# Sums of the density with one factor taken out, and x added on GpSimd, in an attention-then-density kernel

## The chip, the cores and the metric

The kernel runs on one core of a Trainium2 chip. A core has five engines that work side by side, each through its own instructions in order: TensorE (PE; its weight loads are shown as PEld), VectorE (DVE), ScalarE (ACT), GpSimd (POOL) and SyncE (SP), which here issues the DMAs. They wait for each other through semaphores. The metric is the device time of one execution in microseconds; less is better.

## The reference

x has 8 images of 192 channels and 64 x 64 points. Two layers follow each other, each added to x after a group norm (32 groups). The first is attention over the 4096 points of an image, the second a density per channel: a small network of four layers, applied to the normed value less 0.5 and plus 0.5, whose two results give a likelihood.

```python
def _L0_conv_ref(x, w1, b1, a1, w2, b2, a2, wa, ba, aa):
    q, k, v = prelu(conv1x1(x, w1, b1), a1), prelu(conv1x1(x, w2, b2), a2), prelu(conv1x1(x, wa, ba), aa)
    score = softmax(einsum("bnc,bcm->bnm", q, k), axis=2)      # 4096 x 4096 for each image
    return einsum("bnm,bmc->bnc", score, v)

def _logits_cumulative(logits, ms, bs, fs):                    # filters 1, 3, 3, 3, 1 per channel
    for i in range(4):
        logits = einsum("cij,cjn->cin", softplus(ms[i]), logits) + bs[i]
        if i < 3:
            logits = logits + tanh(fs[i]) * tanh(logits)
    return logits

def _L1_conv_ref(x, ...):
    lower, upper = _logits_cumulative(xr - 0.5, ...), _logits_cumulative(xr + 0.5, ...)
    sign = -sign(lower + upper)
    return maximum(abs(sigmoid(sign * upper) - sigmoid(sign * lower)), 1e-6)

x = x + _L0_conv_ref(_gn(x), ...)
x = x + _L1_conv_ref(_gn(x), ...)
```

## The kernel before

**Attention.** An image is cut into 8 blocks of 512 queries, and each block into 16 steps of 256 keys, so an image has 128 steps and the main loop 1024 (`for t in range(last)`). A step issues, in this order: the products and the max-reduce of a step 21 ahead (`max_step`: two matmuls of L753 into the one PSUM tile `mx`, and the reduce L761 on VectorE), the exponential on ScalarE of the next step's scores (L824, L829), and the eight products with the values (`attend`, L840). The next image's norm, keys and values are made in the same steps (`prepare`), and the density of the image before runs beside them. Keys pass through ScalarE and VectorE, then their difference is taken on GpSimd (L613, half as wide as a density piece) and SP stores both to HBM.

**Density.** A tile has 128 partitions and 1024 points. An image makes 12 units (`Unit`): two column blocks c, three channel groups g, two signs s (lower and upper). A unit of images 0 to 6 runs, with tiles from 17 shared buffers:
- `tanh0` (three tanhs of x, L1097) and `linear` (the three linear sums of x of layer 1, L1106) on ScalarE;
- `mix` (9 multiply-adds on VectorE), `tanh` (L1112) and `gate` (3);
- for each of three sums of layer 2: `scaled` on ScalarE (L1122, factor times the first input, plus bias) and `more` twice on VectorE, then tanh, and later the gate;
- for layer 3 `scaled`, one `more`, and `plain` (L1154) on ScalarE, whose result GpSimd adds in two half tiles (L1160).

All multiply-adds but one kind go through the helper `stt`, so they share the line L1129. When both units of a tile are through, `ending` takes the sum, the tanhs (L1354), a sign (L1356), the difference and the product with the sign on GpSimd (L1350, L1362, L1370, in half tiles), the magnitude on ScalarE (L1404), and adds to x on VectorE (L1409).

**Order.** No scheduler of the compiler is used; the program writes the order itself. `density_step` hands out density instructions in each step by planned costs: a rate for VectorE, worked out from the multiply-adds that are left and the steps that are left, and limits by step. It gives an instruction out only when what it needs was given out in an earlier step. GpSimd's half-tile operations wait in the list `pieces`; `pool_step` takes one out in each step and puts a tiny memset (`pause`, L1315) in front, which waits for the last helper multiply-add but one (`recent`), so that the piece runs beside the reduce.

**Tail.** The density of the last image (`on_pe`) runs after the loop, ordered by `tail_step` with planned clocks. The sums of layer 1 are matmuls with diagonal matrices (L1068: three tanhs and x with diagonals of `diagonals` and `linear_diagonals`; `fill` puts x into a bank by ScalarE instead, L1052), then `tanh1` and `gate1` (L1087); layers 2 and 3 are as above. An ending there is all on VectorE and ScalarE (`alone`).

`parameters` works out the constants of the network, one small VectorE operation a step during image 0, and `norm_end` scales them by an image's norm.

Of the kernel before, what the change touches and what calls it, by code (L numbers as in the profile page):

```python
# [18 lines left out]
def kernel(  # L19
# [213 lines left out]
    wx = const.tile([128, 3, 2, 3], F32, name="wx")  # L233
    bx = const.tile([128, 2, 3, 2, 3], F32, name="bx")

    def parameters():
# [30 lines left out]
        yield  # L267
        nc.scalar.activation(tf, ff, AF.Tanh)
# [25 lines left out]
        nc.vector.tensor_copy(wx[:, :, 0, :], wsp[:, :, 0:3])  # L294
        yield
        nc.vector.tensor_copy(wx[:, :, 1, :], la)
        yield
        for i, k in enumerate((-0.5, 0.5)):
            nc.vector.scalar_tensor_tensor(
                bx[:, i, :, 0, :], wsp[:, :, 0:3], k, cb[:, :, 0:3], ALU.mult, ALU.add  # L300
            )
            yield
            nc.vector.scalar_tensor_tensor(bx[:, i, :, 1, :], la, k, lb, ALU.mult, ALU.add)
            yield
# [133 lines left out]
    def norm_end(key, n, t, then=None):  # L438
# [41 lines left out]
        def fourth():  # L480

            res, ve, sq = cell["res"], cell["ve"], cell["sq"]
            rq = small.tile([128, 1], F32, tag="rq", name=f"rq_{nm}")
            nc.vector.reciprocal(rq, sq)
            nc.vector.tensor_tensor(rq, rq, ve, ALU.mult)
            nc.vector.tensor_tensor(rq, rq, sq, ALU.add)
            nc.vector.tensor_scalar(rq, rq, 0.5, None, ALU.mult)
            nc.vector.reciprocal(res[:, 1:2], rq)
            norms[key] = res
            if key[1] == 1:  # L490

                nmr = small.tile([128, 1], F32, tag="nmr", name=f"nmr_{nm}")
                nc.vector.scalar_tensor_tensor(
                    nmr, res[:, 0:1], -1.0, res[:, 1:2], ALU.mult, ALU.mult
                )
                wn = small.tile([128, 3, 2, 3], F32, tag="wn", name=f"wn_{nm}")
                nc.vector.tensor_scalar(wn, wx, res[:, 1:2], None, ALU.mult)
                bn = small.tile([128, 2, 3, 2, 3], F32, tag="bn", name=f"bn_{nm}")
                for i in range(2):
                    nc.vector.scalar_tensor_tensor(  # L500
                        bn[:, i].rearrange("p a b c -> p (a b c)"),
                        wx.rearrange("p a b c -> p (a b c)"), nmr,
                        bx[:, i].rearrange("p a b c -> p (a b c)"), ALU.mult, ALU.add,
                    )
                norms[key] = wn, bn
            if then:
                then()
# [407 lines left out]
    COST = {"DVE": 1.22, "ACT": 1.23, "TANH": 1.05}  # L915
# [6 lines left out]
    lower2 = mm.rearrange("p g n -> p (g n)")[:, 0:36].rearrange("p (s g i) -> p s g i", s=4, g=3)  # L922

    def diagonals(g, t):

        def one(k):
            if k == 0:
                d = vtiles.pop(0).rearrange("p a b c -> p (a b c)")[:, 0 : 12 * 128]
                diag.append(d.rearrange("p (k n) -> p k n", k=12))
            nc.scalar.activation(diag[g][:, k, :], ident, AF.Copy, scale=lc[:, g, k : k + 1])  # L930
# [4 lines left out]
    def linear_diagonals(b, g):  # L935
        wn, bn = norms[b, 1]
        for i in range(3):
            nc.scalar.activation(
                diag[g][:, 9 + i, :], ident, AF.Copy, scale=wn[:, g, 1, i : i + 1]
            )  # L940

    def tail(b):
        wn, bn = norms[b, 1]

        for s in range(2):
            d, q = lower2[:, s], lower2[:, 2 + s]
            nc.vector.tensor_copy(d, cb[:, :, 6:9])
            for j in range(3):
                nc.vector.tensor_tensor(
                    q, wsp[:, :, 12 + j : 21 : 3],  # L950
                    bn[:, s, :, 1, j : j + 1].to_broadcast([128, 3, 3]), ALU.mult,
                )
                nc.vector.tensor_tensor(d, d, q, ALU.add)
# [7 lines left out]
    class Unit:  # L961
# [3 lines left out]
        def __init__(self, b, c, g, s):  # L965
# [29 lines left out]
            else:  # L995
                for i in range(3):
                    add("ACT", ("t", 0, i), [], self.tanh0, makes="t")
                    add("ACT", ("l", 1, i), [], self.linear, makes="l")
                for i in range(3):
                    for j in range(3):  # L1000
                        add(
                            "DVE", ("mix", i, j), [("t", 0, j), ("l", 1, i)], self.mix,
# [5 lines left out]
            for i in range(3):  # L1008
                add("ACT", ("l", 2, i), [("gate", 1, 0)], self.scaled, makes="l")
                for j in (1, 2):  # L1010
                    add("DVE", ("add", 2, i, j), [("gate", 1, j), ("l", 2, i)], self.more)
                add("ACT", ("t", 2, i), [("add", 2, i, 2)], self.tanh, makes="t")
            for i in range(3):
                add("DVE", ("gate", 2, i), [("t", 2, i)], self.gate, frees=[("t", 2, i)])
            add("ACT", ("l", 3, 0), [("gate", 2, 0)], self.scaled, makes="z")
            add("DVE", ("add", 3, 0, 1), [("gate", 2, 1), ("l", 3, 0)], self.more)
            if self.on_pe:
                add("DVE", ("add", 3, 0, 2), [("gate", 2, 2), ("l", 3, 0)], self.more)
            else:

                add("ACT", ("p", 3, 2), [("gate", 2, 2), ("add", 3, 0, 1)], self.plain, makes="p")
# [23 lines left out]
        def fill(self, k):  # L1045
# [4 lines left out]
            if id(banks[0]) in full:  # L1050
# [3 lines left out]
                    scale=norms[b, 1][0][:, g, 1, i : i + 1],  # L1054
                )

        def product(self, k):
# [6 lines left out]
            for n, src in enumerate([self.src()] + [self.buf["u", 0, j] for j in range(3)]):  # L1064
                if n == 0 and filled:
                    continue
                for h in range(2):
                    nc.tensor.matmul(  # L1068
                        out[:, h, :], lhsT=diag[g][:, 3 * i + n - 1 if n else 9 + i, :],
# [4 lines left out]
        def tanh1(self, k):  # L1074
# [4 lines left out]
                bias=norms[b, 1][1][:, s, g, 1, i : i + 1],  # L1079
            )  # L1080

        def gate1(self, k):
# [5 lines left out]
                dst, dst, tf[:, g, 3 + i : 4 + i], src, ALU.mult, ALU.add  # L1088
# [3 lines left out]

        def tanh0(self, k):
            b, c, g, s = self.key
            wn, bn = norms[b, 1]
            i = k[2]
            nc.scalar.activation(  # L1097
                self.buf[k], self.src(), AF.Tanh, bias=bn[:, s, g, 0, i : i + 1],
                scale=wn[:, g, 0, i : i + 1],
            )  # L1100

        def linear(self, k):
            b, c, g, s = self.key
            wn, bn = norms[b, 1]
            i = k[2]
            nc.scalar.activation(  # L1106
                self.buf[k], self.src(), AF.Identity, bias=bn[:, s, g, 1, i : i + 1],
                scale=wn[:, g, 1, i : i + 1],
            )

        def tanh(self, k):
            nc.scalar.activation(self.buf[k], self.buf["l", k[1], k[2]], AF.Tanh)  # L1112

        def scaled(self, k):
            g, s = self.key[2:]
            n, i = k[1], k[2]
            w = 3 + 9 * (n - 1) + 3 * i
            if self.on_pe and n == 2:
                offset = lower2[:, s, g, i : i + 1]
            else:  # L1120
                offset = cb[:, g, 3 * n + i : 3 * n + i + 1]
            nc.scalar.activation(  # L1122
                self.buf[k], self.buf["l", n - 1, 0], AF.Identity,
                bias=offset, scale=wsp[:, g, w : w + 1],
            )

        def stt(self, dst, src, factor):
            recent.append(
                nc.vector.scalar_tensor_tensor(dst, src, factor, dst, ALU.mult, ALU.add)  # L1129
            )  # L1130

        def mix(self, k):
            g, i, j = self.key[2], k[1], k[2]
            self.stt(self.buf["l", 1, i], self.buf["t", 0, j], lc[:, g, 3 * i + j : 3 * i + j + 1])

        def gate(self, k):
            g, n, i = self.key[2], k[1], k[2]
            f = 3 * n + i
            self.stt(self.buf["l", n, i], self.buf["t", n, i], tf[:, g, f : f + 1])

        def more(self, k):
            g, n, i, j = self.key[2], *k[1:]
            w = 3 + 9 * (n - 1) + 3 * i + j
            self.stt(self.buf["l", n, i], self.buf["l", n - 1, j], wsp[:, g, w : w + 1])
            if (n, i, j) == (2, 2, 2):
                for q in range(3):
                    self.give(("l", 1, q))
            if (n, j) == (3, 2):
                self.end()

        def plain(self, k):
            g = self.key[2]
            src, dst, z = self.buf["l", 2, 2], self.buf[k], self.buf["l", 3, 0]
            nc.scalar.activation(dst, src, AF.Copy, scale=wsp[:, g, 23:24])  # L1154
# [21 lines left out]
        def need(self):  # L1176
            most = dict(self.left, t=max(0, min(self.left["t"], 1 - self.held["t"])))
            if ("add", 2, 2, 2) not in self.at:
# [27 lines left out]
        def give_out(self, eng, t, when):  # L1206
# [6 lines left out]
            elif eng == "ACT":  # L1213
                took = 0.97 if self.quick(name) else 1.13
# [9 lines left out]
        def quick(self, name):  # L1224
            return name[0] == "t" and name[1] or self.on_pe and name[:2] == ("l", 1)

        def step(self, eng, t, older):
            todo = self.todo[eng]
            while todo and credit[eng] > 0:
                name, after, fn, makes, frees = todo[0]  # L1230
                if any(self.at.get(a, t) >= t for a in after if eng != "DVE" or a[0] in "ltu"):
# [3 lines left out]
                cost = COST["TANH" if name[0] == "t" and name[1] else eng]  # L1235
# [58 lines left out]
    def density(b):  # L1294
        if b == B - 1:
            linear_diagonals(b, 0)
            for g in (1, 2):
                at(now[0] + 3 * g, lambda g=g: linear_diagonals(b, g), 0.0, 1.2)
            at(now[0] + 1, lambda: tail(b), 2.2)
# [10 lines left out]
    def pool_step():  # L1310


        if pieces:
            if len(recent) == 2:
# [10 lines left out]
    def ending(b, c, g):  # L1325


        z = [zs.pop((b, c, g, i)) for i in range(2)]
        halves = [slice(h * F, h * F + F) for h in range(2)]
# [22 lines left out]
        def tanhs(h):  # L1352
            for i in range(2):
                nc.scalar.activation(z[i][:, halves[h]], z[i][:, halves[h]], AF.Tanh, scale=0.5)  # L1354
            s = cell["s"][:, halves[h]]
            nc.scalar.activation(s, s, AF.Sign)  # L1356
# [15 lines left out]
        def alone():  # L1372
# [12 lines left out]
            def second():  # L1385
                for n in parts:
                    for i in range(2):
                        nc.scalar.activation(z[i][:, n], z[i][:, n], AF.Tanh, scale=0.5)
# [247 lines left out]
```

## Time and profile before

| | |
|---|---|
| median of 3 runs | 4580.5 us (4580.42 to 4583.0) |
| profiled execution, its own time | 4580.02 us |
| its span, first to last instruction | 4578.2 us |
| granted TensorE clock, mean | 0.985 |
| busy: PE, DVE, ACT, POOL | 4310.9, 4118.3, 3228.2, 962.1 us |
| multiply-adds of the helper (L1129) | 1980, 2539 us busy |
| max-reduces (L761) from `mx` | 1003, 1221.2 us |
| GpSimd's density pieces (L1160, L1350, L1362, L1370) | 408 |

Times of engines are busy times in one profiled execution; a busy TensorE is not a TensorE at its peak, since its matmuls are pipelined. The 1.8 us between span and time lie around the program. A line of a group shows line, engine, operation, the tile written and those read, count, busy time and mean, then the idle time of the engine just before, and what ended it. In a timeline a line that merges several instructions shows their number at its end.

### The profile page before, as it was taken

Reading aid. Unit: us, or ns where it says so; the run is one execution under the profiler, and the core shown is the slowest. Engines: PE = TensorE matmul, PEld = TensorE weight load, DVE = VectorE, ACT = ScalarE, POOL = GpSimd, SP = SyncE. Lnnn points to the kernel's source line nnn. Section 1 sums busy time; section 2 is a strip of 40 time slices with the busy share of each in tenths; the row PEclk is TensorE's granted clock in tenths of the full one; section 3 lists DMA queues with packets and bytes.
Section 4 is the critical chain, followed back from the end, with each engine's and each line's share of the span. In section 5 each row is a group of like instructions: output and inputs, shape, how many; then the busy total and the mean of one; then the engine's idle time right before and its main releaser. Section 6 shows DMA issues by size and latency. Waiting matters only on the chain.

```text
span 4578.2 us, 60221 instructions
## 1 busy us (share of the span) xinstructions
PE 4310.9 (94%) x23640; PEld 3803.1 (83%) x23640; DVE 4118.3 (90%) x4270; ACT 3228.2 (71%) x3699; POOL 962.1 (21%) x904
## 2 busy tenths in 40 slices
PE   7999999999999999999999999999999999999685
PEld 5999998898988888888888888888888889888232
DVE  4433369999999999999999999999999999999898
ACT  2333347776778777777777777787778777778786
POOL 1000002222123221322222312232223232222100
PEclk8999999999999999999999999999999999999898
DMA  3101221113200221113111221103111121000000
GB/s 82 42 20 38 46 53 28 34 30 71 47 26 24 61 51 35 34 36 64 32 37 39 47 65 33 30 25 65 42 43 34 31 54 27 9 11 19 9 14 14
DMA packets 199468, 171.96 MB, mean 38 GB/s; under 512 B 86544, under 2 KB 160144, under 8 KB 199184
## 3 DMA queue, kind: packets, MB, share of 16 engines
q1 hardware_dynamic: 198112, 167.64, 15.9%
q8 instruction: 186, 3.05, 0.3%
q14 instruction: 98, 0.80, 0.1%
q10 hardware_dynamic: 1072, 0.47, 0.1%
HBM read 125.84 MB, written 42.21 MB: 37 GB/s over the span
## 4 chain that ended last, share of the span: by engine, by line
DVE 67%; PE 18%; ACT 7%; issue 6%; POOL 1%; DMA 1%; SPq 0%; POOLq 0%; DVEq 0%; ACTq 0%
DVE d L1129 41%; DVE rm L761 18%; PE b L840 10%; PE sc L824 2%; PE mx L753 2%; DVE st L436 2%; ACT d L1122 1%; PE b L1068 1%; ACT e L829 1%; ACT d L1112 1%; ACT d L1097 1%; DVE v L722 1%; DVE xc L885 1%; PE b L709 1%; DVE xc L1409 1%
## 5 line engine op out<-in xcount | busy, mean ns | idle before, releaser
L840 PE MATMUL b<-v,e 128*128 128x193 f32 x16384 | 2848.0, 327 | 0.1
L840 PEld LDWEIGHTS b<-v,e 128*128 128x128 f32 x16384 | 2732.6, 190 | 90.9 <-DVE xc L885 0.6
L829 ACT ACTIVATE e<-sc 128x1024 f32<-128x1024 f32 x1024 | 1041.0, 1017 | 820.9 <-PE sc L824 818.8
L761 DVE TENSOR_REDUCE rm<-mx 128x1 f32<-128x1024 f32 x1003 | 1221.2, 1218 | 331.8 <-PE mx L753 331.2
L1129 DVE SCALAR_TENSOR_TENSOR d<-d,lc,d 128x1024 f32<-128x1024 f32 x756 | 977.0, 1301 | 13.8 <-ACT d L1097 2.0
L1129 DVE SCALAR_TENSOR_TENSOR d<-d,wsp,d 128x1024 f32<-128x1024 f32 x684 | 879.8, 1289 | 44.1 <-ACT d L1122 34.9
L824 PE MATMUL sc<-q,kr 98*128 98x512 f32 x2048 | 776.5, 460 | 38.1 <-ACT e L829 30.4
L753 PE MATMUL mx<-kr,q 96*128 96x512 f32 x2006 | 659.4, 410 | 94.5 <-DVE rm L761 90.7
L1112 ACT ACTIVATE d<-d 128x1024 f32<-128x1024 f32 x540 | 565.9, 1052 | 202.3 <-DVE d L1129 201.1
L1129 DVE SCALAR_TENSOR_TENSOR d<-d,tf,d 128x1024 f32<-128x1024 f32 x540 | 682.5, 1287 | 1.8 <-ACT d L1112 1.8
L1315 POOL MEMSET pause<- 128x1 f32 x408 | 40.0, 98 | 2755.5 <-DVE d L1129 2755.5
L753 PEld LDWEIGHTS mx<-kr,q 96*128 96x128 f32 x2006 | 354.4, 189 | 271.5 <-DVE rm L761 205.2
L1122 ACT ACTIVATE d<-d,cb,wsp 128x1024 f32<-128x1024 f32 x348 | 429.1, 1234 | 18.2 <-DVE d L1129 15.6
L824 PEld LDWEIGHTS sc<-q,kr 98*128 98x128 f32 x2048 | 349.2, 191 | 89.5 <-ACT e L829 52.9
L1160 POOL TENSOR_TENSOR d<-d,d 128x512 f32<-128x512 f32 x168 | 354.8, 2112 | 14.7 <-ACT d L1154 13.9
L1097 ACT ACTIVATE d<-xc,bn,wn 128x1024 f32<-128x1024 f32 x288 | 354.0, 1234 | 1.2 <-DVE bn L500 1.2
L1106 ACT ACTIVATE d<-xc,bn,wn 128x1024 f32<-128x1024 f32 x252 | 311.3, 1235 | 0.0
L613 POOL TENSOR_TENSOR kq<-kq,kh 128x256 f32<-128x256 f32 x64 | 74.1, 1159 | 556.4 <-ACT kh L610 556.4
L1350 POOL TENSOR_TENSOR d<-d,d 128x512 f32<-128x512 f32 x80 | 173.8, 2173 | 0.2 <-issue 0.2
L1370 POOL TENSOR_TENSOR d<-d,d 128x512 f32<-128x512 f32 x80 | 169.5, 2119 | 1.9 <-POOL pause L1315 0.6
L1362 POOL TENSOR_TENSOR d<-d,d 128x512 f32<-128x512 f32 x80 | 158.5, 1981 | 0.0
L1354 ACT ACTIVATE d<-d 128x512 f32<-128x512 f32 x160 | 92.0, 624 | 93.0 <-POOL d L1350 71.2
(174 smaller groups left out, 2290.6 us busy)
## 6 DMA issues: line engine op xcount, KB each, us to landing
xi<-in_x_dram SPq DMA_DIRECT2D x280, 192.0 KB
kr<-kqd SPq DMA_DIRECT2D x296, 96.0 KB
xc<-in_x_dram SPq DMA_DIRECT2D x64, 384.0 KB
out_dram<-xc SPq DMA_DIRECT2D x94, 256.0 KB
q<-kqd SPq DMA_DIRECT2D x128, 96.0 KB
kqd<-kh SPq DMA_DIRECT2D x64, 128.0 KB
kqd<-kq SPq DMA_DIRECT2D x64, 128.0 KB
d<-in_x_dram SPq DMA_DIRECT2D x16, 192.0 KB
```

The lines of the kernel that those rows point to most:

```text
L753: nc.tensor.matmul(sc[:, s, :], lhsT=tile_of(qt[b, n // 2], n, j)[0 : 4 * CR].bitcast(F32R), rhs=keys_of(b, c)[0 : 4 * CR, s, :].bitcast(F ...
L761: nc.vector.tensor_reduce(out=rowmax[b, n][:, j, k : k + 1], in_=sc, axis=AX.XY, op=ALU.max)
L824: nc.tensor.matmul(sc[:, s, :], lhsT=keys_of(b, ORDER[p // 4])[r, s, k : k + 128].bitcast(F32R), rhs=qt[b, n // 2][r, :, u : u + 256].bitc ...
L829: return lambda: nc.scalar.activation(e, sc, AF.Exp)
L840: nc.tensor.matmul(a[:, j, 0 : C + 1], lhsT=e[:, s, j * 128 : j * 128 + 128], rhs=v[:, s, p % 4, :], start=p == 0 and s == 0 and j % 2 == ...
L1097: nc.scalar.activation(self.buf[k], self.src(), AF.Tanh, bias=bn[:, s, g, 0, i : i + 1], scale=wn[:, g, 0, i : i + 1],)
L1106: nc.scalar.activation(self.buf[k], self.src(), AF.Identity, bias=bn[:, s, g, 1, i : i + 1], scale=wn[:, g, 1, i : i + 1],)
L1112: nc.scalar.activation(self.buf[k], self.buf["l", k[1], k[2]], AF.Tanh)
L1122: nc.scalar.activation(self.buf[k], self.buf["l", n - 1, 0], AF.Identity, bias=offset, scale=wsp[:, g, w : w + 1],)
L1129: nc.vector.scalar_tensor_tensor(dst, src, factor, dst, ALU.mult, ALU.add)
L1160: return nc.gpsimd.tensor_tensor(z[:, n], z[:, n], dst[:, n], ALU.add)
L1350: return nc.gpsimd.tensor_tensor(cell["s"][:, n], z[0][:, n], z[1][:, n], ALU.add)
```

## The change

Each sum of layers 1 to 3 is kept divided by one of its factors, and that factor goes into the scale (with the bias) of the next tanh. The offsets of all layers move into the biases of the tanhs.
- Layer 1 (`begin`): the first tanh times its constant is made on ScalarE, then GpSimd adds x to it in two half tiles, and two `mix` multiply-adds follow for each sum (6 a unit, where 9 were). `linear` goes.
- Layers 2 and 3 (`two`, `third`): a sum is first input times a ratio plus second input, and then that times a ratio plus the third, both on VectorE. `scaled` goes; layer 3 keeps its `plain` outside the tail.
- The tanhs of layers 1 and 2, the ending's tanhs and its sign get a scale and a bias by pointer.
- `pool_step` takes two pieces out where more than three wait, with one pause in front of both.
- In the tail one diagonal for x (the norm's factor alone) replaces nine, `tail` no longer works out offsets, and an ending in the tail has one Identity activation more.
- `parameters` makes the new constants, `norm_end` scales more of them. The planned costs of the tanhs on ScalarE become the common ones.

```diff
+    wx = const.tile([128, 3, 10], F32, name="wx")
+    bx = const.tile([128, 2, 3, 10], F32, name="bx")
+    sr = const.tile([128, 3, 10], F32, name="sr")
+    si = const.tile([128, 3, 15], F32, name="si")
+    rt = const.tile([128, 3, 8], F32, name="rt")
...
+                wn = small.tile([128, 3, 10], F32, tag="wn", name=f"wn_{nm}")
+                nc.vector.tensor_scalar(wn, sr, res[:, 1:2], None, ALU.mult)
+                un = small.tile([128, 3, 15], F32, tag="un", name=f"un_{nm}")
+                nc.vector.tensor_scalar(un, si, rq, None, ALU.mult)
...
-    COST = {"DVE": 1.22, "ACT": 1.23, "TANH": 1.05}
+    COST = {"DVE": 1.22, "ACT": 1.23}
...
     def tail(b):
...
+        res = norms[b, 1][4]
+        nc.scalar.activation(diag[0][:, 9, :], ident, AF.Copy, scale=res[:, 1:2])
...
                     add("ACT", ("t", 0, i), [], self.tanh0, makes="t")
-                    add("ACT", ("l", 1, i), [], self.linear, makes="l")
+                    if i == 0:
+                        for k in range(3):
+                            add(
+                                "ACT", ("l", 1, k), [("t", 0, 0)], self.begin, makes="l",
+                                frees=[("t", 0, 0)] if k == 2 else [],
+                            )
                 for i in range(3):
-                    for j in range(3):
+                    for j in (1, 2):
                         add(
-                            "DVE", ("mix", i, j), [("t", 0, j), ("l", 1, i)], self.mix,
+                            "DVE", ("mix", i, j), [("t", 0, j), ("x", i)], self.mix,
                             frees=[("t", 0, j)] if i == 2 else [],
                         )
...
             for i in range(3):
-                add("ACT", ("l", 2, i), [("gate", 1, 0)], self.scaled, makes="l")
-                for j in (1, 2):
-                    add("DVE", ("add", 2, i, j), [("gate", 1, j), ("l", 2, i)], self.more)
-                add("ACT", ("t", 2, i), [("add", 2, i, 2)], self.tanh, makes="t")
+                add("DVE", ("l", 2, i), [("gate", 1, 1)], self.two, makes="l")
+                add("DVE", ("add", 2, i), [("gate", 1, 2)], self.third)
+                add("ACT", ("t", 2, i), [("add", 2, i)], self.tanh, makes="t")
...
-            add("ACT", ("l", 3, 0), [("gate", 2, 0)], self.scaled, makes="z")
-            add("DVE", ("add", 3, 0, 1), [("gate", 2, 1), ("l", 3, 0)], self.more)
+            add("DVE", ("l", 3, 0), [("gate", 2, 1)], self.two, makes="z")
...
+        def begin(self, k):
             b, c, g, s = self.key
             i = k[2]
+            dst, x_ = self.buf[k], self.src()
             nc.scalar.activation(
+                dst, self.buf["t", 0, 0], AF.Copy, scale=norms[b, 1][1][:, g, 3 * i : 3 * i + 1]
+            )
+
+            def add(h):
+                n = slice(h * F, h * F + F)
+                if h == 1:
+                    self.at["x", i] = now[0] + 1
+                return nc.gpsimd.tensor_tensor(dst[:, n], dst[:, n], x_[:, n], ALU.add)
+
+            pieces.append(lambda: add(0))
+            pieces.append(lambda: add(1))
...
+        def two(self, k):
+            g, n, i = self.key[2], k[1], k[2]
+            f = i if n == 2 else 6
+            self.stt(
+                self.buf[k], self.buf["l", n - 1, 0], rt[:, g, f : f + 1], self.buf["l", n - 1, 1]
+            )
...
     def pool_step():
 
 
-        if pieces:
-            if len(recent) == 2:
+        for n in range(2 if len(pieces) > 3 else 1):
+            if not pieces:
+                return
+            if len(recent) == 2 and n == 0:
                 inst = nc.gpsimd.memset(pause, 0.0)
...
-            nc.scalar.activation(s, s, AF.Sign)
+            nc.scalar.activation(s, s, AF.Sign, bias=offset[2], scale=half)
...
                 for n in parts:
                     for i in range(2):
-                        nc.scalar.activation(z[i][:, n], z[i][:, n], AF.Tanh, scale=0.5)
+                        y = z[i][:, n]
+                        nc.scalar.activation(y, y, AF.Tanh, bias=offset[i], scale=half)
+                    y = s[:, n]
+                    nc.scalar.activation(y, y, AF.Identity, bias=offset[2], scale=half)
                 later(2, third, 2.5)
```

## The prediction

> **What bounds the kernel now.** Read first the page's busy shares, its 40 slices and the chain that ended last:
>
> ```profile
> PE 4310.9 (94%) x23640; PEld 3803.1 (83%) x23640; DVE 4118.3 (90%) x4270; ACT 3228.2 (71%) x3699; POOL 962.1 (21%) x904
> ...
> DVE  4433369999999999999999999999999999999898
> ACT  2333347776778777777777777787778777778786
> POOL 1000002222123221322222312232223232222100
> ...
> DVE 67%; PE 18%; ACT 7%; issue 6%; POOL 1%; DMA 1%; SPq 0%; POOLq 0%; DVEq 0%; ACTq 0%
> ```
>
> TensorE has the larger sum, but from the seventh slice on VectorE is full and the chain runs through it. Next read the busy times cut at the images (stretches between the first exponentials of L829 of each image, 128 steps each): the columns are time, then PE, PEld, DVE, ACT, POOL. Image 0 has no density work, a middle image has it, the last row is the tail.
>
> ```profile
> 103.50:596.10 492.60, 491.49 (x2826) 460.62 (x2826) 197.01 (x274) 162.75 (x212) 5.80 (x8) 0.99 0.18 39
> 596.10:1110.70 514.60, 503.86 (x2885) 461.48 (x2885) 482.73 (x502) 379.56 (x436) 109.66 (x98) 1.00 0.18 41
> 2164.10:2692.30 528.20, 508.39 (x2885) 460.10 (x2885) 523.19 (x535) 406.87 (x466) 138.75 (x129) 1.00 0.18 42
> 3747.60:4232.30 484.70, 464.79 (x2589) 426.15 (x2588) 473.62 (x454) 382.70 (x432) 130.61 (x120) 1.00 0.08 16
> 4232.30:4578.30 346.00, 235.94 (x530) 103.21 (x528) 302.35 (x278) 254.15 (x250) 12.65 (x12) 0.86 0.05 12
> ```
>
> Image 0 is TensorE's own pace, 492.6 us with VectorE at 197. A middle image takes 528.2, and VectorE is busy for 523.2 of it. So VectorE sets the middle, and the most that any relief of it can bring there is 528.2 - 492.6 = 35.6 us an image.
>
> Last, how GpSimd and VectorE meet. The timeline of both engines, beside a max-reduce and then where two multiply-adds of the helper L1129 follow each other:
>
> ```profile
> 2001.40 2.60 DVE L1129 SCALAR_TENSOR_TENSOR d<-d,wsp,d 128x1024 f32<-128x1024 f32 x2
> 2002.86 2.27 POOL L1350 TENSOR_TENSOR d<-d,d 128x512 f32<-128x512 f32 x1
> 2003.92 1.22 DVE L761 TENSOR_REDUCE rm<-mx 128x1 f32<-128x1024 f32 x1
> ...
> 4171.29 1.27 DVE L1129 SCALAR_TENSOR_TENSOR d<-d,lc,d 128x1024 f32<-128x1024 f32 x1
> 4171.55 2.15 POOL L1350 TENSOR_TENSOR d<-d,d 128x512 f32<-128x512 f32 x1
> 4172.49 2.29 DVE L1129 SCALAR_TENSOR_TENSOR d<-d,tf,d 128x1024 f32<-128x1024 f32 x1
> ...
> 4213.47 1.27 POOL L1160 TENSOR_TENSOR d<-d,d 128x512 f32<-128x512 f32 x1 [3.56 <-ACT d L1154]
> ```
>
> With VectorE waiting, GpSimd adds half a tile in 1.27 us. Started during a multiply-add it takes 2.15 to 2.27: it stands until the multiply-add ends, and then works. If a reduce (from PSUM) follows, that costs VectorE nothing, the reduce stays at 1.22. If another multiply-add follows, this one grows from 1.27 to 2.29. A GpSimd piece is free beside a reduce and costs VectorE 0.9 to 1.03 us between two multiply-adds (the 2.29 less 1.27; others read 2.31 and, at 4237.9, 2.20). The pause (L1315) waits for the last multiply-add but one so that a piece falls beside the reduce.
>
> **VectorE's saving.** A unit before the tail had 9 mixes, 3 gates, 6 adds, 3 gates and 1 add: 22. It will have 6 + 3 + 6 + 3 + 1 = 19, since the first mix term starts the sum on ScalarE and x comes in on GpSimd. 84 units make 252 multiply-adds fewer. In the middle image the helper's 265 took 334.2 us of busy time, 1.26 each: 252 x 1.26 = 318 us, 45 in a middle image (36 of them).
>
> **GpSimd's new work, and its price.** Each unit adds 6 half-tile pieces, 504 in all; pieces go from 408 to some 908, in a middle image from 60 to 132, and with the half-size key differences to 140, for 128 reduces. In the changed kernel's order of instructions 597 groups stand behind a pause; 311 of them hold two density pieces. The first of a pair falls beside the reduce as now. The second stands behind it and takes the port after the first multiply-add of the next step. Of the 128 steps of a middle image, 68 issue two multiply-adds and 19 three: in 87, 68%, another one follows and pays. In the rest it slides beside the next reduce; but the six pieces of a unit come as pairs in successive steps, so I count 4 in 10 of those as pushing out the next first piece: 0.68 + 0.32 x 0.4 = 0.8. So 311 x 0.8 x 0.95 = 236 us comes back on VectorE. Bounds: with every reduce used, only 140 - 128 = 12 pieces an image pay, 11 us; with every second piece paying 1.03 us, it is 320 us, the whole saving. I take 236, as the rows with a following multiply-add are nearest to two thirds of the steps.
>
> In a sentence apart: the Trainium skill, GPSIMD Engine Reference, section 4.1 (Engine selection), advises against elementwise adds on GpSimd, about twice as slow as VectorE for two inputs; 504 x 1.27 against 252 x 1.26 us shows that ratio here, and by the rule the adds stay where they are and the main saving is nought. It weighs engines one by one, while here GpSimd is 21% busy.
>
> Who waits for GpSimd: every multiply-add that needs an x add stands at least two steps, some 8 us, behind it in the order, and a pair with its wait is under 5 us, so I put this wait at nothing. If GpSimd falls a step behind, VectorE stands up to 1.3 us with the reduce queued behind it, and TensorE's next max product behind that. GpSimd's key differences (L613) queue behind up to two pieces, and the queue SP, which stores them, with its loads behind; keys are used the image after, so some 4 us are covered by that image.
>
> **ScalarE.** Out: 3 linear terms and 4 scaled ones a unit, at 1.235; in: 3 starts (like the plain scaling, 1.14); 6 tanhs go from 1.05 to 1.23 with two pointers. That is 4.1 us less a unit. An ending gains 6 x 0.18. ScalarE stands 818.8 us for scores, so no time either way in the main part.
>
> **Small edits.** parameters() has some 38 more VectorE operations of 0.17 us, one a step in image 0, where VectorE is idle 60%; uncovered they would cost 7 us. The wider norm constants and the two more (un, ds) are under 1 us an image, 7 in all.
>
> Main part: -318 + 236 + 7 = -75. A middle image loses 45 - 33 - 1 = 11 and goes to 517, still above TensorE's 492.6, so the whole counts.
>
> **The tail.** Here the multiply-adds stay 14 a unit, but the scaled terms leave the path. VectorE is busy 302.35 of 346 us, and most of its idle time is one wait, in this group of the stretch 4232.3 to 4578.3:
>
> ```profile
> L1129 DVE SCALAR_TENSOR_TENSOR d<-d,wsp,d 128x1024 f32<-128x1024 f32 x111 | 142.4, 1285 | 29.8 <-ACT d L1122 27.6
> ```
>
> L1122 is the scaled start of layers 2 and 3, which becomes a multiply-add waiting only for gates on VectorE's own queue. What is late next is a tanh or TensorE's sum (235.9 busy of 346). Between none of the 27.6 and all of it I take 20, since only 1.8 us now waits for the tanhs (L1112). tail()'s VectorE operations of 2.3 us and eight of nine diagonals of 0.39 on ScalarE go: -4. The last ending gains two half-size Identity activations and pointers: +2. Tail -22.
>
> Sum: -75 - 22 = -97. The profiled execution took 4580.0 (span 4578.2 and 1.8 around it), against a median of 4580.5: 4483 us. About 9 us, 0.2%, is what a measurement of this kernel can tell from no change.
>
> **Rivals.** The forecast, 50%: with 0.65 to 0.95 of the 311 second pieces paying and a tail of -28 to -10, 4433 to 4540. *TensorE's floor*, 15%: pairs find idle or reduces, 12 pieces an image pay. A middle image would be 528 - 45 + 12 = 495, held near 498 with today's 5 us of idle: 30 x 5, 16 for image 1 (514.6), 24 for the last, 190, with the tail 4368. For it: VectorE idles once TensorE is the slower. Against: 12 needs perfect placing. *Break-even*, 17%: all 311 pay 1.03; the main part gives nothing, the tail 20 or less: 4560; a quarter of this case lies within 0.2%. *GpSimd's pieces lose the reduce*, 13%, the slower one: first pieces too start at any time, because an x piece waits for its start on ScalarE in the same or the last step, as L1160 waits for L1154 (13.9 us now, 12 times). Its place is the middle images. Saving and tail, 318 + 22 - 7 = 333 us, are spent at 350 paying pieces of 908; with one in four of 597 first ones beside the 249, 398 pay 378 us: +45, 4625; with half of them, over 4760. Against: only 12 waits in 84 today. *Doing nothing*, 5%: VectorE's relief reappears as waits for tanhs and scores, about 4578.
>
> Faster: 0.50 + 0.15 + three quarters of 0.17 = 0.78; same 0.05; slower 0.13 and the last of break-even, 0.17. For eight in ten the range runs from 4390, into the floor case, to 4600, into the slower one; the forecast's own is 4430 to 4540.
>
> **What would show it.** Right: the helper's multiply-adds 252 fewer; middle images near 517 with VectorE still about 99% busy; the mean multiply-add up from 1.28 (2539 us over 1980) to about 1.42, as 236 us spreads over 1728; reduces unchanged at 1.22; no VectorE wait for ScalarE's scaled term in the tail. Wrong: middle images at 495 (the pieces hide) or above 528 (first pieces pay as well), VectorE waiting for the x adds, or a tail not shorter than 335.

## The result, and the profile after

The changed kernel takes 4612.65 us (median of 4 runs, 4610.19 to 4614.02), the kernel before on the same chip 4581.36: a ratio of 1.0067, 95% interval 1.005 to 1.0085. It is 31 us slower, where 97 us less was forecast. The profiled execution has a span of 4611.4 us.

**The page.** First the busy times, the slices of VectorE and GpSimd, and the chain that ended last:

```profile
PE 4321.9 (94%) x23640; PEld 3846.8 (83%) x23640; DVE 4053.9 (88%) x4058; ACT 2925.5 (63%) x3316; POOL 1840.1 (40%) x1597
...
DVE  4444369999999999999999999999999999999999
...
POOL 1000024453446535555454544454354554454300
...
DVE 48%; PE 40%; DMA 4%; issue 3%; ACT 3%; POOL 2%; SPq 1%; DVEq 0%; POOLq 0%; ACTq 0%
```

VectorE has 64 us less to do, ScalarE 303 us less, and yet the span grew by 33. In the chain VectorE's share went from 67% to 48%, TensorE's from 18% to 40%, and the DMAs' from 1% to 4%. VectorE no longer sets the whole middle, though its slices still read 9: a digit of 9 hides up to a tenth of idle time.

**The same stretches as before**, cut at the first exponential of each image. Columns: time, then PE, PEld, DVE, ACT, POOL, the granted clock, the DMA share, GB/s.

```profile
102.70:595.30 492.60, 491.49 (x2826) 460.60 (x2826) 201.37 (x312) 162.62 (x212) 5.81 (x8) 0.99 0.18 39
595.40:1118.00 522.60, 506.16 (x2885) 465.50 (x2884) 478.17 (x473) 351.20 (x400) 234.60 (x204) 0.99 0.19 41
2187.40:2722.90 535.50, 509.95 (x2885) 466.99 (x2884) 512.01 (x501) 368.53 (x418) 265.56 (x227) 0.99 0.20 42
3795.30:4302.40 507.10, 469.06 (x2596) 436.87 (x2595) 475.89 (x424) 350.47 (x390) 261.85 (x219) 0.97 0.10 15
4302.40:4611.40 309.00, 232.73 (x522) 101.43 (x521) 290.67 (x258) 202.53 (x187) 11.67 (x13) 0.88 0.05 14
```

In the middle image VectorE is busy for 512.0 us. That is the forecast's figure to the microsecond (523.2 - 45 + 33 + 1). But the image took 535.5, not 517: VectorE idles 23.5 us in it, where it idled 5.0 before. Image 1 is 8 us longer than before, the five middle images together 40 and the last one 22.4; the tail is 37.0 shorter. So what has to be explained is the idle time of an engine that is 96% busy.

**The groups** of the page with the multiply-adds and reduces:

```profile
L1204 DVE SCALAR_TENSOR_TENSOR d<-d,un,d 128x1024 f32<-128x1024 f32 x1008 | 1467.1, 1477 | 6.2 <-ACT d L1198 1.9
...
L847 DVE TENSOR_REDUCE rm<-mx 128x1 f32<-128x1024 f32 x1003 | 1221.0, 1217 | 472.1 <-PE mx L839 471.3
...
L1204 DVE SCALAR_TENSOR_TENSOR d<-d,rt,d 128x1024 f32<-128x1024 f32 x684 | 904.2, 1335 | 5.3
...
L910 PE MATMUL sc<-q,kr 98*128 98x512 f32 x2048 | 780.0, 462 | 94.8 <-DMA q<-nd 59.6
L1190 POOL TENSOR_TENSOR d<-d,xc 128x512 f32<-128x512 f32 x504 | 955.4, 1909 | 309.2 <-ACT d L1182 308.9
```

The multiply-adds grew from a mean of 1.28 us to 1.40 (2371.3 over these 1692), and the reduces stayed at 1217 ns. The two waits that grew stand behind the bars: reduces that wait for TensorE's max products (471.3 us; 331.2 before), and score products that wait for the DMA `q<-nd` (59.6; 5.9 before). Of the 308.9 us ahead of GpSimd's adds, 239.0 are one wait, for the first of them at 655 us, when nothing else was there to do.

**The second wait on SP's timeline.** `nd<-rn` is the store of a block's row maxima, `q<-nd` their read into the rows of the queries. First before, then after, both at block 6 of an image, counted from 0 (columns: start, duration, engine, line, operation, count):

```profile
2016.78 0.37 SPq L795 DMA_DIRECT2D nd<-rn  x1
...
2026.93 0.67 SPq L799 DMA_DIRECT2D q<-nd  x1
2029.93 1.17 SPq L1423 DMA_DIRECT2D out_dram<-xc  x2
2033.68 2.83 SPq L97 DMA_DIRECT2D xc<-in_x_dram  x4
```

```profile
2033.81 0.37 SPq L881 DMA_DIRECT2D nd<-rn  x1
2034.23 1.22 SPq L1513 DMA_DIRECT2D out_dram<-xc  x2
...
2045.84 2.53 SPq L97 DMA_DIRECT2D xc<-in_x_dram  x4
2048.49 0.64 SPq L885 DMA_DIRECT2D q<-nd  x1
```

The order on SP has turned round. Before, the read of the maxima goes first, and then the output of a finished density tile and the load of the next tile of x. After, the output and the load stand between store and read. The load goes into the tile that the output is read from, so it waits for that store to land: in this stretch SP's wait `SPq L97 <- DMA out_dram<-xc` is 10.3 us, where it is 2.5 in the stretch of before. The read waits behind it, and the scores of block 6 wait for the read. The tile there is (c, g) = (0, 2), whose ending comes in another step now. This happens seven times, once in each of images 2 to 6 and twice in the last (at blocks 2 and 6), and each time the scores wait for 6.6 to 8.1 us.

### The profile page after: what moved, and what is told of

It is laid out like the page before. It is cut to its first block, busy times and chain, and to the rows that moved or that the text cites. A ratio compares the mean times of both kernels' runs of the same rounds, so it can differ in the third digit from the quotient of the medians.

```text
span 4611.4 us, 60314 instructions
## 1 busy us (share of the span) xinstructions
PE 4321.9 (94%) x23640; PEld 3846.8 (83%) x23640; DVE 4053.9 (88%) x4058; ACT 2925.5 (63%) x3316; POOL 1840.1 (40%) x1597
## 4 chain that ended last, share of the span: by engine, by line
DVE 48%; PE 40%; DMA 4%; issue 3%; ACT 3%; POOL 2%; SPq 1%; DVEq 0%; POOLq 0%; ACTq 0%
DVE d L1204 30%; PE b L926 25%; DVE rm L847 12%; PE sc L910 5%; PE mx L839 5%; PE b L795 3%; DMA out_dram<-xc 1%; DMA q<-nd 1%; PE b L678 1%; DVE st L522 1%; DVE xc L1499 1%; DVE d L1159 1%; DVE v L808 1%; ACT d L1441 1%; POOL d L1436 1%
## 5 line engine op out<-in xcount | busy, mean ns | idle before, releaser
L926 PEld LDWEIGHTS b<-v,e 128*128 128x128 f32 x16384 | 2761.6, 191 | 91.5
L847 DVE TENSOR_REDUCE rm<-mx 128x1 f32<-128x1024 f32 x1003 | 1221.0, 1217 | 472.1 <-PE mx L839 471.3
L1204 DVE SCALAR_TENSOR_TENSOR d<-d,un,d 128x1024 f32<-128x1024 f32 x1008 | 1467.1, 1477 | 6.2 <-ACT d L1198 1.9
L1190 POOL TENSOR_TENSOR d<-d,xc 128x512 f32<-128x512 f32 x504 | 955.4, 1909 | 309.2 <-ACT d L1182 308.9
L1204 DVE SCALAR_TENSOR_TENSOR d<-d,rt,d 128x1024 f32<-128x1024 f32 x684 | 904.2, 1335 | 5.3
L910 PE MATMUL sc<-q,kr 98*128 98x512 f32 x2048 | 780.0, 462 | 94.8 <-DMA q<-nd 59.6
L1198 ACT ACTIVATE d<-d,bn,wn 128x1024 f32<-128x1024 f32 x504 | 619.1, 1237 | 115.7 <-DVE d L1204 107.0
L1173 ACT ACTIVATE d<-xc,bn,wn 128x1024 f32<-128x1024 f32 x288 | 351.5, 1235 | 13.2 <-DVE bn L588 13.2
L1246 POOL TENSOR_TENSOR d<-d,d 128x512 f32<-128x512 f32 x168 | 311.9, 1869 | 21.9 <-ACT d L1240 20.6
L1182 ACT ACTIVATE d<-d,un 128x1024 f32<-128x1024 f32 x252 | 278.5, 1141 | 0.0
L1441 ACT ACTIVATE d<-d,bn,wn 128x512 f32<-128x512 f32 x160 | 121.3, 806 | 80.1 <-POOL d L1436 66.2
L1449 POOL TENSOR_TENSOR d<-d,d 128x512 f32<-128x512 f32 x80 | 161.4, 2018 | 0.0
L1457 POOL TENSOR_TENSOR d<-d,d 128x512 f32<-128x512 f32 x80 | 158.0, 1976 | 4.1 <-POOL pause L1397 0.3
L1436 POOL TENSOR_TENSOR d<-d,d 128x512 f32<-128x512 f32 x80 | 153.5, 1926 | 0.3 <-issue 0.3
L795 PE MATMUL b<-wv,xi 64*128 64x192 f32 x1344 | 139.5, 340 | 0.7 <-ACT v L805 0.7
```

Source lines behind the costliest of these rows:

```text
L795: nc.tensor.matmul(pv[:, s, 0:C], lhsT=t[p, g, k * 128 : k * 128 + 128] if g < 3 else one_row[p], rhs=wf["v", b][p, g, :] if g < 3 else wf ...
L847: nc.vector.tensor_reduce(out=rowmax[b, n][:, j, k : k + 1], in_=sc, axis=AX.XY, op=ALU.max)
L910: nc.tensor.matmul(sc[:, s, :], lhsT=keys_of(b, ORDER[p // 4])[r, s, k : k + 128].bitcast(F32R), rhs=qt[b, n // 2][r, :, u : u + 256].bitc ...
L926: nc.tensor.matmul(a[:, j, 0 : C + 1], lhsT=e[:, s, j * 128 : j * 128 + 128], rhs=v[:, s, p % 4, :], start=p == 0 and s == 0 and j % 2 == ...
L1173: nc.scalar.activation(self.buf[k], self.src(), AF.Tanh, bias=bn[:, s, g, i : i + 1], scale=wn[:, g, i : i + 1],)
L1182: nc.scalar.activation(dst, self.buf["t", 0, 0], AF.Copy, scale=norms[b, 1][1][:, g, 3 * i : 3 * i + 1])
```

## The experiments

Two theories stand for the main part. One: SP's order stalls TensorE some 8 us an image. Two: GpSimd's pairs of pieces cost more than VectorE's time, since they fall in successive steps. Against them stood that the x adds' starts or the planner make the loss. Of these, a wait for the x adds can be read off the groups above: of the 6.2 us of idle time ahead of the multiply-adds with `un`, which need them, 1.9 are put down to ScalarE and none to GpSimd, so the forecast's nothing for this wait held. The kernel before took 4579.59 us beside the first four experiments and 4581.15 beside the last three.

**Load later.** The changed kernel, but no load of x is issued while a block's row maxima are between their collection and their read:

```
+ waiting = [0]                      # max_end: += 1 ahead of at(now[0], collect, 0.4)
+                                    # spread:  -= 1 after made.add(("max", b, n))
- if free[kind] > 0 and kind not in held:
+ if free[kind] > 0 and kind not in held and not (kind == "xc" and waiting[0]):
```

> The changed kernel, with the load of the next x tile held back while the row maxima of a block (the store to nd and the read back into q) are on their way, so that on SP the read into q stands ahead of that load again, as in the kernel before. Theory SP: in seven images the read into q stood behind the load, which waited for an output store, and the scores of block 6 came 8 us late: 4612 - 7 x 8 = 4556, and the step at the start of block 6 falls from 12.3 us to about 4. Rival GpSimd: the loss comes from the second pieces and from waits for the x adds, and the step at block 6 is only where it shows: 4612 within 10.

4555.55 us (median of 5), ratio to before 0.9946 (0.9933 to 0.9958): 57 us less than the changed kernel, as its theory had it. SP's timeline of this kernel, where block 6's read now precedes the load:

```profile
2026.22 0.37 SPq L882 DMA_DIRECT2D nd<-rn  x1
2026.65 1.22 SPq L1516 DMA_DIRECT2D out_dram<-xc  x2
...
2037.18 0.67 SPq L886 DMA_DIRECT2D q<-nd  x1
2038.26 2.56 SPq L97 DMA_DIRECT2D xc<-in_x_dram  x4
```

The score products' wait for `q<-nd` fell from 59.6 us to 9.6 (8 times). No arithmetic was changed, so the 57 us were SP's order. The other experiments on the changed kernel stand on this one, and are compared with its 4555.55.

**Before, with the load first.** The reverse, in the kernel before: the output of tile (0, 2) two steps earlier, and block 6's read one step later, so that its order on SP is that of the changed kernel.

```
- at(now[0] + 3, spread)
+ at(now[0] + (4 if n == 6 else 3), spread)
- at(now[0] + 2, send)
+ at(now[0] + (0 if (c, g) == (0, 2) else 2), send)
```

> The kernel before, with the output of one tile of an image sent two steps earlier and the read of block 6's row maxima into q one step later, so that in six images the load of the next x tile stands ahead of that read on SP, as in the changed kernel. Nothing of the density is touched. Theory SP: six stalls of 6 to 9 us, 4581 + 45 = 4626. Rival GpSimd: without the x adds on GpSimd the order on SP costs nothing, 4581.

4648.44 us, ratio 1.0151 (1.0135 to 1.0166): 69 us slower than before, where 45 was expected. Its list of waits (after the colon: total us, times, the longest) have the stall by itself:

```profile
PE sc L824 <- DMA q<-nd: 70.8, 8, 11.1
```

These are six stalls of 10 to 11 us, against 7 to 8 in the changed kernel, and SP's timeline at block 6 shows why they are longer:

```profile
2027.99 0.37 SPq L795 DMA_DIRECT2D nd<-rn  x1
2041.14 1.14 SPq L1423 DMA_DIRECT2D out_dram<-xc  x2
2044.86 2.53 SPq L97 DMA_DIRECT2D xc<-in_x_dram  x4
2047.80 0.66 SPq L799 DMA_DIRECT2D q<-nd  x1
```

The output now stands in the list ahead of the add to x that makes it, so SP waits 12.7 us for VectorE (L1409) before the store and 2.5 for it after, and the read begins 19.8 us behind the store of the maxima, where it was 14.7 in the changed kernel. So SP's order costs this with no x add and no changed arithmetic, though it isn't the same stall: what its own later step, some 4 us, costs the read is not separated.

**No x add.** Load later, with the 504 adds of x on GpSimd left out; x is then missing from the sums of layer 1.

```
- pieces.append(lambda: add(0))
- pieces.append(lambda: add(1))
+ self.at["x", i] = now[0] + 1
```

> As the first kernel of this call, and the adds of x in layer 1 on GpSimd are left out (504 half-tile pieces; x is missing from the sums). Second pieces fall from 311 to 41. Theory port: the multiply-adds go back from a mean of 1.42 to about 1.29, VectorE's busy time in a middle image from 512 to about 480, and a middle image falls to TensorE's pace and today's idle time, 497: some 30 us in each of six images and 15 in the last below the first kernel, 4556 - 195 = 4360. Rival: TensorE and the queues set the middle images whatever GpSimd does, and the time stays within 40 us of 4556.

4374.68 us, ratio 0.9554 (0.9541 to 0.9567): 181 us less than load later, 15 above the theory's 4360, and far from the rival's 4556. Load later is 24 us faster than before, and its tail alone is 36 us shorter (309.9 against 346.0), so its main part brings nothing: the adds, on an engine that is 41% busy, take back all that the dropped multiply-adds bring there. The row of a middle image, first of load later and then of this kernel:

```profile
2169.60:2699.00 529.40, 507.80 (x2885) 464.89 (x2884) 512.72 (x501) 368.36 (x418) 264.55 (x227) 0.99 0.20 42
```

```profile
2098.90:2602.30 503.40, 498.85 (x2885) 463.14 (x2884) 489.74 (x502) 367.86 (x418) 128.64 (x124) 1.00 0.21 44
```

VectorE does the same 501 or 502 operations in 23 us less, which is the price in its busy time; the image is 26 us shorter, and at 503.4 it is TensorE's, busy for 498.9 of it.

**Layer 3's last term on VectorE.** Load later, with the last term of layer 3 a multiply-add in every unit, not only in the tail. That is 84 multiply-adds more and 168 pieces fewer.

```
- if self.on_pe:
-     add("DVE", ("add", 3, 0), [("gate", 2, 2)], self.third)
- else:
-     add("ACT", ("p", 3, 2), [("gate", 2, 2), ("l", 3, 0)], self.plain, makes="p")
+ add("DVE", ("add", 3, 0), [("gate", 2, 2)], self.third)
```

> As the first kernel of this call, and the last term of layer 3 is a multiply-add on VectorE in all units, as it is in the tail, in place of a scaling on ScalarE and an add of two half-tile pieces on GpSimd: 84 multiply-adds more, 168 pieces fewer, second pieces from 311 to 226. Theory port: a piece that stands second costs 0.8 x 0.95 us, so 85 of them are 65 us against 84 x 1.26 = 106 us more: 4556 + 41 = 4597, or no change if the pieces beyond one a reduce all pay (168 x 0.65 = 109). Rival: GpSimd's queue itself, its 140 pieces an image, is what delays: 4556 - 40.

4545.59 us, ratio 0.9926 (0.9913 to 0.994): 10 us less than load later, between the two expectations. 168 pieces for 84 multiply-adds is about an even trade as long as the pieces go in pairs; it decides nothing. VectorE is busy 516.7 us of an image of 526.5.

**Pairs only over 7.** Load later, with one number changed: a step issues a second piece only when more than 7 are queued, not 3. The same 912 pieces are done, but 92 of them as second ones, where it was some 311.

```
- for n in range(2 if len(pieces) > 3 else 1):
+ for n in range(2 if len(pieces) > 7 else 1):
```

> The kernel with the load held back, and two pieces are taken out in a step only where more than 7 wait, not more than 3: second pieces fall from 311 to 92, the 908 pieces stay. Theory port in bursts: a second piece makes its step longer by about 1 us and the pairs stand in successive steps, so TensorE waits there for the reduce, and in the light steps VectorE waits for TensorE (17 and 14 us in a middle image of 529). 219 pairs fewer at 0.8 x 0.95 are 166 us on VectorE, and most of it counts, since a middle image with VectorE at 489 would be held at about 503 as without the x adds: 4556 - 140 = 4415 within 30. Rival total work: GpSimd's 140 pieces for 128 reduces cost the same wherever they stand, and the time stays at 4556 within 15. Rival late x: the x adds come later, the multiply-adds wait for them, over 4560.

4431.73 us, ratio 0.9677 (0.9662 to 0.9691): 124 us less than load later, for the same work, and within the expectation. The row of a middle image:

```profile
2126.40:2636.20 509.80, 500.81 (x2886) 462.87 (x2885) 498.32 (x501) 367.98 (x419) 276.29 (x259) 1.00 0.19 43
```

VectorE's busy time is 14.4 us less than in load later's image, and the image is 19.6 shorter: pairs cost VectorE busy time, and 5 us of idling on top. Over images 1 to 7 together it is 104 us of busy time and 20 of idle time. The waits of a middle image tell where the idling was, first in before, then in load later, then here:

```profile
PEld mx L753 <- DVE rm L761: 33.7, 45, 1.5
...
PE mx L753 <- DVE rm L761: 15.2, 26, 1.0
```

```profile
PEld mx L839 <- DVE rm L847: 27.6, 26, 2.7
...
PE mx L839 <- DVE rm L847: 17.4, 20, 2.2
...
DVE rm L847 <- PE mx L839: 14.3, 18, 4.4
```

```profile
DVE rm L847 <- PE mx L839: 8.4, 14, 1.2
...
PEld mx L839 <- DVE rm L847: 6.6, 10, 1.8
```

(Columns as above.) In before TensorE waits for the reduces often and briefly, and VectorE's wait for TensorE's products is at most 0.5 us. In load later each engine waits for the other by turns in one image. TensorE waits for the reduce that frees `mx` (its weight load 27.6 us, the product 17.4), fewer times than in before but up to 2.7 us at once, in steps that pairs have made long; and VectorE waits for TensorE's product (14.3), in steps where it has little. Counted from reduce to reduce, 41 of the image's 128 steps have at most one multiply-add of the helper, and they hold 12.8 of VectorE's 16.7 us of idle time; before had 22 such steps, with 0.8 us. Without most of the pairs both waits shrink.

**Pairs only over 9.** The same with 9; 62 second pieces.

> As the kernel with pairs over 7, with pairs over 9: 62 second pieces in place of 92. Theory port in bursts: 30 pairs fewer, 20 us less at most, 5 to 20 below the one over 7. Rival late x: the longer queue of pieces makes the x adds late, the planner gives the multiply-adds out later and denser, and the time is above the one over 7.

4454.49 us, ratio 0.9725 (0.9709 to 0.9742): 23 us more than with 7, so the forecast was missed and its rival's time came. The row shows what turned:

```profile
2134.20:2646.20 512.00, 501.18 (x2885) 462.56 (x2884) 490.66 (x501) 368.51 (x418) 280.62 (x263) 1.00 0.19 44
```

VectorE is busy for 7.7 us less than with 7, as fewer pairs should make it, but the image is 2.2 us longer: it idles 21.3. In a middle image 10 steps now have no multiply-add (4 with 7) and 22 have three (20). The list of work is less even, so fewer pairs are no longer better here; that the late x adds make it so, as the rival says, is not shown.

**Layer 3's last term on VectorE, and never two pieces.** The edit of the fourth experiment, with `> 12` for the pairs; its 744 pieces then all go singly.

> The kernel with the load held back and layer 3's last term on VectorE, and never two pieces in a step: 740 pieces, no second one. Theory port in bursts: the 84 multiply-adds more cost 106 us, the 226 second pieces of the run with that term on VectorE are gone, 226 x 0.76 = 172 us on VectorE: 4546 - 150 = 4396 within 30, near the kernel with pairs over 7, less or more by 20. Rival total work: 4546 within 15.

4429.23 us, ratio 0.9667 (0.9653 to 0.9681), 3 us above the expected range. Its rival, that single pieces bring nothing here, would have left 4546. The row of a middle image:

```profile
2119.90:2628.90 509.00, 500.52 (x2885) 462.76 (x2884) 498.78 (x513) 356.06 (x406) 234.11 (x225) 1.00 0.21 44
```

It reads like that of pairs over 7, by another road. Its multiply-adds show what single pieces still cost:

```profile
L1203 DVE SCALAR_TENSOR_TENSOR d<-d,un,d 128x1024 f32<-128x1024 f32 x1008 | 1310.9, 1324 | 6.3 <-ACT d L1197 3.3
...
L1203 DVE SCALAR_TENSOR_TENSOR d<-d,rt,d 128x1024 f32<-128x1024 f32 x768 | 1000.4, 1316 | 6.1
```

These lie 77 us above an undisturbed 1.277 us each. Both versions are some 150 us faster than before, 3.3% and 3.2%, and the 2.5 us between them can't be told apart.

## Why the prediction was wrong, point by point

**Multiply-adds and their count: right.** The counts went as the step had it: 252 fewer, and the helper's are 1692, with 36 in the tail beside them. VectorE's saving and the price that GpSimd takes back together left 512.0 us in the middle image, as forecast. Image 1 and the last are another matter (below).

**GpSimd's price: the sum nearly right, its split not.** The 1008 multiply-adds of 1.477 and 684 of 1.335 lie 1008 x 0.200 + 684 x 0.058 = 241 us above the undisturbed 1.277 (the mean of those of before that took under 1.35). Before had 32 of such excess, so the change added some 209 us, against 236 forecast. The reduces stayed at 1.217. But the forecast put all of it on second pieces, at 0.8 x 0.95 = 0.76 us each. From load later to pairs over 7 this excess falls from 243 to 130 us with 219 second pieces fewer, 0.52 each; between the two runs with layer 3's last term on VectorE it falls from 172 to 77 with 226 fewer, 0.42 each. And 744 single pieces cost 77 us, not nothing. That the sum came out is in part luck. The timeline after shows the mechanism that the prediction took from before:

```profile
674.76 3.48 DVE L1204 SCALAR_TENSOR_TENSOR d<-d,un,d 128x1024 f32<-128x1024 f32 x2
674.79 2.37 POOL L1190 TENSOR_TENSOR d<-d,xc 128x512 f32<-128x512 f32 x1
677.15 2.21 POOL L1190 TENSOR_TENSOR d<-d,xc 128x512 f32<-128x512 f32 x1
...
678.17 1.21 DVE L847 TENSOR_REDUCE rm<-mx 128x1 f32<-128x1024 f32 x1
```

Two multiply-adds take 3.48 us with a piece between them, the second of its pair, where two take 2.60 in the timeline of before; the next piece then falls beside the reduce, which keeps its 1.21.

**"Still above TensorE's 492.6, so the whole counts": wrong, and the largest miss, about 85 us.** The step compared VectorE's sum for a whole image with TensorE's sum for a whole image. But the two are tied in each step, by the reduce that frees `mx` and the product that fills it. Pieces come six to a unit, and go in pairs in successive steps; these steps become longer than TensorE's, and TensorE waits. The steps with few multiply-adds, of which there are 41 for 22, are TensorE's, and VectorE waits there. So of a forecast gain of 11 us an image, load later shows none: its images 2 to 6 take 527.1 on average, those of before 527.4. Load later's own rows give the size: (527.1 - 517) x 5 = 50; and, with the forecast's 11 taken off the times of before in image 1 and the last, 522.7 - 503.6 = 19 and 489.4 - 473.7 = 16.

Some 67 us of it is idle time: over images 1 to 7 VectorE idles 136 us in load later and 69 in before. The rest is VectorE's own sum, which fell by 10.6 us in an average image of 2 to 6, as forecast, but only by 5 in image 1, and rose by 2 in the last. Of the idle time, pairs over 7 shows that the pairs make some 20 us: the same pieces, spread over more steps, bring 124 us, of which 104 are VectorE's busy time, the price that the forecast had in its sum. The other 47 stay open: the way in which the list spreads multiply-adds has a part in such idling, since pairs over 9 idles 177 us with fewer pairs still, but no run separates this further.

The floor was too low as well. Image 0 has 2826 matmuls in its row and a middle image 2885, and without the x adds, when TensorE set the pace, a middle image took 503.4 us, not 492.6.

**"Who waits for GpSimd": the wrong queue was walked, 57 us.** That paragraph followed SP only for the keys. The ending of a density tile moves too, and with it two entries in SP's list: the output's store and the load that waits for it. The read `q<-nd` was in the list a few entries away, with TensorE's scores behind it. No term of the sum stood for it, though the order of the four entries is fixed by the program and needs no run to be read. Load later shows it by taking it out, and before with the load first shows that such an order costs time in the old kernel too (69 us).

**The tail: right in kind, 15 us better than its term.** The wait for the scaled start went wholly, where 20 of 27.6 was taken. VectorE's busy time fell from 302.4 to 290.7 us, where 4 was taken, and its idle time from 43.6 to 18.3. Some 9 us of the busy time are no saving of the tail itself: seven multiply-adds fewer of image 6's density fall into this stretch (the helper has 164 in it, for 171), and the forecast counts that image's in the main part. The multiply-adds there, mean 1.285 before, are

```profile
L1204 DVE SCALAR_TENSOR_TENSOR d<-d,rt,d 128x1024 f32<-128x1024 f32 x110 | 140.2, 1290 | 1.7
```

with 1.7 us of idle time ahead of them for 29.8. So the step was right that nothing else is close behind; the 8 us it held back for a next wait were not needed.

**The sum.** 4483 + 57 (SP) + 85 (the main part) - 15 (the tail) = 4610; 4612.65 was measured.

**The rivals.** *GpSimd's pieces lose the reduce* has the sign of the result, but not its mechanism: single pieces do pay, but the price of all of them was no higher than the forecast's. Its sign, a middle image above 528, came (535.5) for other reasons. *TensorE's floor* and *break-even* both argued about that price, and its sum was right. *Doing nothing* named waits for scores, which came, but by way of a DMA list that it did not name. What was missing was a rival in which VectorE's sum falls as forecast and the image does not.

## What to carry to other kernels

When two engines are tied to each other in every step, a saving is worth only what it takes out of the steps that the slower engine sets: compare them step by step, and before moving work to an idle engine ask in which steps it will land, since the same work in bursts cost 124 us more than spread, most of it as longer instructions of the busy engine. When a change shifts when a buffer is finished, read the new order of every DMA list that serves it; one load that waits for a store, in front of a small read that TensorE needs, cost 57 us with no arithmetic in it. A forecast of an engine's busy time in a stage can be right to the microsecond and the time still wrong: say as well where its idle time will be.

## What was unexpected of the hardware

That a store, a load into the same tile and a small read in one SP list make a chain of waits: the load stood 10.3 us for the store (2.5 in the stretch of before; why the store takes longer here is open), and the read of the maxima began 14.7 us after its store, where it was 10.2 before (2048.49 less 2033.81; 2026.93 less 2016.78). And that the price falls on either engine: GpSimd's pieces have a mean of 1909 ns, where one alone took 1.27 us, and without the x adds the same 1008 multiply-adds have a mean of 1320 ns, with 92 second pieces 1377, and with some 311 of them 1479, at an unchanged number of pieces for the last two:

```profile
L1206 DVE SCALAR_TENSOR_TENSOR d<-d,un,d 128x1024 f32<-128x1024 f32 x1008 | 1309.7, 1320 | 11.8 <-ACT d L1200 7.2
```

```profile
L1207 DVE SCALAR_TENSOR_TENSOR d<-d,un,d 128x1024 f32<-128x1024 f32 x1008 | 1368.8, 1377 | 6.3 <-ACT d L1201 1.8
```

```profile
L1207 DVE SCALAR_TENSOR_TENSOR d<-d,un,d 128x1024 f32<-128x1024 f32 x1008 | 1469.0, 1479 | 6.2 <-ACT d L1201 1.9
```

They are, in this order, the groups of no x add, of pairs over 7 and of load later.
